# Four fused layers in one kernel: another port rule in its planner, shift by single elements, shared buffers, a maximum as Relu

## The chip, the core and the metric

The kernel runs on one core of a Trainium2 chip. A core has five engines that run their own instruction streams and wait for each other with semaphores: TensorE (PE, with weight loads shown apart as PEld), VectorE (DVE), ScalarE (ACT), GpSimd (POOL), and SyncE (SP), which here only issues transfers. The metric is the device time of one execution in microseconds; of several executions the median.

## What is computed

32 images `x` of 256 x 256 go through four layers, one after the other, each with its own weights. Cut to what matters:

```python
# layer 0: norm over the whole image, scale and shift by a condition, silu, two 256x256 products, residual
# layer 1: token norm with condition, attention of 16 heads with a bias per head, feed-forward of 1024
h = _ln(src) * (1.0 + scale) + shift
scores = einsum('bhqd,bhkd->bhqk', q / sqrt(16), k) + attention_bias      # fside, 32 x 16 x 256 x 256
scores = where(src_mask, -inf, scores); ctx = softmax(scores) @ v
x = x + (ctx @ Wo + bo)
return x + _gelu2(_ln(x) * g2 + beta2 @ W1 + b1) @ W2 + b2
# layer 2: a finite-difference step on the image as a grid
df = -gradv_Af + gradvv_Bf * 0.5
return maximum(f + df * dt, 0.0)
# layer 3: layer norm, causal attention of 16 heads, feed-forward with exact gelu, gated residual
x1 = x + attn(layernorm(x)); x2 = x1 + ff(layernorm(x1))
return x + gate_score * (x2 - x)
```

`_ln(x)` is `(x - mean) / sqrt(var + 1e-5)` along a row. All numbers are fp32.

## The kernel before

An image lies on chip as a tile of 128 partitions x 2 x 256. For each image three generators describe its work: `layer_0`, `layer_1`, and `layers_23` (the grid step and the last layer). They don't issue instructions. A recorder, class `Order`, notes each call with its engine, its operands and a due time (its rank); a step of a generator (`yield LAND` and the like) moves the due time on by so many microseconds times `PACE`, and `PERIOD`, `START`, `EDGE` and `SHIFT` place images, layers and steps against each other. When everything is noted, `arrange` plays the program through with a model of the engines: at each moment it gives each engine, among its units that are ready by the model, the one of the lowest rank. `emit` then issues all calls in the order of the planned starts. So the order on every engine is fixed in the program; the chip runs each engine's stream in that order. Work of two to three images is interleaved.

The model (lines 72 to 90 and `length`) has a duration for each form of instruction, the hop from one engine to another (`HOPS`, `OWNS`, and `SLACK`, a margin for TensorE), what a change of TensorE's shape costs (`TURN`, `FIRST`), how many PSUM banks scores, transposes and products may hold (`CAPS`), and the port: a unit marked `port` on VectorE can't run beside one on GpSimd. `record` sets the mark by the number of elements of the operands (16 and more).

The tiles that matter here:
- `sc`: scores of one head in PSUM. VectorE's fused operation adds the bias (`nb` in layer 1, prepared by GpSimd from the loaded `fside` and the mask; `causal` in layer 3), writes `pr` and the row's minimum `mn`. ScalarE turns `pr` into exponentials and sums them. TensorE transposes `pr` into `tr`, VectorE or ScalarE copies that to `pt`, and TensorE multiplies `pt` by the values. `pr` has six buffers for layer 1 (`pr1`) and six for layer 3 (`pr3`).
- `ctx_t`: the product with the values, copied by ScalarE, then multiplied by VectorE with the inverse sums, which GpSimd spreads (`wide`) and TensorE transposes. Then comes `L1wo` or `L3wo`.
- `token_norm` (used twice in each attention layer): VectorE takes mean and variance into `mv`, GpSimd computes `rstd` with a power, VectorE makes `shift` (-mean x rstd, two columns), ScalarE writes the normalised tile (`t` in the profile, as the tag `t2`), which TensorE transposes.
- `xm` (layer 1 after attention) and `d` (layer 3) have one buffer each; `d` is stored to memory at the end of an image.
- `x` at the end of layer 2 ("x3"): `dd * dt + f` on VectorE, then the maximum with zero, also on VectorE, then `token_norm`.

All transfers but a few at the start are issued by SyncE, in the planned order too.

Of the kernel before, what the change touches and what calls it, by code (L numbers as in the profile page):

```python
# [21 lines left out]
P = 128  # L22
# [19 lines left out]
PERIOD = 86.0  # L42
START = (-59.8, 0.0, 116.9)
PACE = (1.37, 1.22, 1.08)
EDGE = {(0, 0): -102.4, (0, 1): -3.5, (0, 2): 0.3, (1, 0): -29.2, (1, 1): -9.5, (1, 2): -3.3, (2, 0): -4.4, (2, 1): -1.3, (2, 2): 1.9, (3, 0): 7.5, (3, 2): 0.7, (4, 0): -2.3, (4, 1): 1.2, (4, 2): 0.6, (27, 0): 7.3, (27, 1): 1.5, (27, 2): 0.7, (28, 0): -2.3, (28, 1): 1.6, (28, 2): 4.6, (29, 0): 2.1, (29, 1): -0.7, (29, 2): -0.1, (30, 0): 0.1, (30, 1): 3.4, (30, 2): -0.3, (31, 0): 3.1, (31, 1): 3.6, (31, 2): -30.9}
SHIFT = (
    {0: -23.5, 1: -31.5, 2: -24.4, 3: -36.5, 4: -13.4, 5: -35.7, 6: -44.8, 7: -28.5, 8: 20.9},
    {0: -11.9, 1: -93.5, 2: -5.9, 3: 2.4, 4: 4.1, 5: 6.4, 7: -9.2, 8: 7.3, 9: -92.1, 11: 7.2, 12: 20.9,
     13: -0.6, 14: 4.6, 15: -3.0, 16: 12.9, 17: 7.8, 19: 5.4, 20: 7.9, 21: 35.0, 22: 16.8, 23: -7.6,
     24: -11.1, 25: -25.5, 26: -3.5, 27: -66.1, 28: -0.5, 29: -110.6, 30: -4.3, 31: -15.2, 32: -19.4,  # L50
     33: 1.6, 34: -0.4, 35: 12.9, 36: 0.6, 37: -15.0},
    {0: -3.0, 1: -43.2, 2: 3.0, 3: 26.5, 4: 23.8, 5: -31.8, 6: -42.4, 7: -14.5, 8: -8.2, 9: 6.5,
     11: 3.8, 12: 16.4, 13: -29.4, 15: -3.4, 16: 18.0, 17: -4.1, 18: 7.0, 19: 0.1, 20: 0.7, 21: -69.9,
     23: 8.3, 24: 7.8, 25: -0.5, 26: -13.8, 27: -43.4, 28: 14.4, 29: -5.3, 30: 25.3, 31: 1.7, 32: -8.7,
     33: -40.0, 34: 13.4, 35: -21.0, 36: -92.3, 37: -36.5, 38: -60.7, 39: 56.2, 40: -26.9, 41: 7.7},
    {0: -11.5, 1: 3.4, 2: -31.6, 3: -95.1, 4: 57.5},
)
# [7 lines left out]
class Order:  # L65
# [8 lines left out]
    SETUP = 15e3  # L74
    HOPS = {"act": 40.0, "dve": 40.0, "pool": 90.0, "pe": 60.0, "sync": 60.0}
    OWNS = {"act": 30.0, "dve": 30.0, "pool": 83.0, "sync": 30.0}
    TURN = 92.0
    FIRST = {(32, P): 107.0, (P, 32): 27.0}
    SLACK = 50.0
    SEEN = 165.0  # L80
    CAPS = {"sc": 6, "tr": 7, "mm": 6}
    EARLIER = {"sc": 28.7, "mm": -1.9, "tr": 6.1}
    STAY = 5.0
    PORT = 0.05
# [41 lines left out]
    def record(self, engine, call, method, args, kwargs):  # L126
# [11 lines left out]

        inner = [a for a in ins if math.prod(n for _, n in a.ap[1:]) >= 16]
        sources = sum(a.space != PSUM for a in inner)  # L140
        alone = method in ("tensor_scalar", "tensor_copy") and all(a.space != PSUM for a in outs)
        x["port"] = bool(inner) and (engine == "pool" or engine == "dve" and (sources > 1 or sources == 1 and alone))
        x["lead"] = 142.0 if engine == "pool" else x["length"][2] if engine == "dve" else 0.0
# [24 lines left out]
    def length(self, engine, method, outs, ins, args, kwargs):  # L168
# [5 lines left out]
        if engine == "pe":  # L174
            lhs = kwargs.get("lhsT")
            rows = 32 if lhs is not None and lhs.partition_size() <= 32 else P
            cols = 32 if outs[0].partition_size() <= 32 else P
            slot = (lhs.start_partition(), outs[0].start_partition()) if lhs is not None else (0, 0)
            passes = 1 if method == "transpose" or kwargs.get("is_transpose") else 2
            one = max(free(outs[0]) / 1.2 + 2.3, 109.0) if free(outs[0]) > 16 else 70.0  # L180
            return one * passes, (rows, cols), slot
        if method == "dma_start":
            return sum(math.prod(k for _, k in a.ap) for a in outs) * 4
        if engine == "dve":
            lead = 137.0
            if method == "reciprocal":
                return 120 + 8.3 * n, 40 + 8.3 * n, lead
            if method == "tensor_tensor_reduce":
                return 235 + 1.05 * n, 73 + 1.05 * n, lead
            if method == "tensor_scalar":  # L190
                a = (265 if columns else 150) + (1.06 if psum else 0.55) * n
                lead = 257.0 if columns else lead
            elif method == "scalar_tensor_tensor":
                a = 205 + 1.05 * n
                lead = 195.0
            else:
                a = 148 + 1.05 * n
            return a, a - 80, lead
        if engine == "act":
            if method == "copy":  # L200
                a = 157 + 0.84 * n
            else:
                a = (255 if columns else 200) + 0.84 * n + (93 if columns > 1 else 0)
                if "accum_out" in kwargs:
                    a += 115
            return a, a - 95, self.TABLES.get(args[2] if len(args) > 2 else None)
        if method == "tensor_tensor":
            a = 640 if n <= 4 else 185 + 2.13 * n
        else:
            a = 185 + 0.86 * n + (70 * columns if columns > 1 else 0)  # L210
        return a, a - 40 if n > 4 else a + 10

    def arrange(self):
# [47 lines left out]
        banks = defaultdict(lambda: (None, 0.0))  # L261
        table = None

        def may(u, at):
# [11 lines left out]
        while todo:  # L276
# [6 lines left out]
            for e in self.ENGINES:  # L283
# [6 lines left out]
                for k, heap in ready[e].items():  # L290
# [5 lines left out]
                    if e == "pe" and units[u][2][0]["length"][1] != shape:  # L296
                        rank += self.STAY
                    if k[1]:
                        rank += self.PORT * max((pool_end if e == "dve" else dve_end) - now, 0.0)
# [10 lines left out]
                for x in units[u][2]:  # L310
                    if e == "pe":
                        one, its_shape, slot = x["length"]
                        if its_shape != shape:
                            t = max(t, pe_end + self.TURN)
# [5 lines left out]
                        x["start"] = pe_last = t  # L320
                        done = t + one + (0.0 if slot in slots else self.FIRST.get(shape, 0.0))
                        slots[slot] = done
                        pe_end = max(pe_end, done)
                        t = done if shape == (P, P) else t + 6.6
                        done += self.SEEN
                    elif x["method"] == "dma_start":
# [3 lines left out]
                    else:  # L330
                        x["start"] = now
                        more = max((pool_end if e == "dve" else dve_end) - now - x["lead"], 0.0) if x["port"] else 0.0
                        more = max([more] + [t - now for f, t in map(banks.__getitem__, x["banks"]) if f != e])
                        if e == "act" and x["length"][2] not in (None, table):
                            table = x["length"][2]
                            more += self.TABLE
                        done, t = (now + a + more for a in x["length"][:2])
                        if x["port"] and e == "pool":
                            pool_end = done
# [74 lines left out]
def kernel(ctx: ExitStack, tc: tile.TileContext, io, out, n_batch=B):  # L414
# [23 lines left out]
    causal = ctile("causal", [P, S])  # L438
    edge = ctile("edge", [P, 3, 2, 4])

# [128 lines left out]

    small = sb.tile([P, 16, B], F32, tag="pr1", name="encodings", bufs=6)  # L570
    x0, r0, n0, a0, enc, x1f, r1, n1, a1, emb0, emb1 = (small[:, i] for i in range(11))
# [35 lines left out]

    small = sb.tile([P, 4, 4, B], F32, tag="pr1", name="hidden0", bufs=6)
    h1, zh, th, h1s = (small[:, i] for i in range(4))
    small = sb.tile([P, 4, 4, B], F32, tag="pr1", name="hidden1", bufs=6)  # L610
    h2, zh1, th1, embs = (small[:, i] for i in range(4))
# [70 lines left out]
    def loads():  # L682

        load_rest(l1, "L1", "g2", "beta2")
        yield LAND

        sync.dma_start(edge, io["c_edge"].rearrange("p (k e x) -> p k e x", k=3, e=2))
        a1 = sb.tile([P, C2, D], F32, tag="l2", name="a1", bufs=4)
# [37 lines left out]
    def token_norm(x, tag="t2", bufs=3):  # L726

        st = sb.tile([P, C2, 6], F32, tag="st", name="st", bufs=4)
        mv = sb.tile([P, C2, 2], F32, tag="mv", name="mv", bufs=4)
# [4 lines left out]
        shift = sb.tile([P, C2], F32, tag="shift", name="shift", bufs=4)  # L734
        dve.scalar_tensor_tensor(shift, mv[:, :, 0], -1.0, r, ALU.mult, ALU.mult)
        xn = sb.tile([P, C2, D], F32, tag=tag, name=tag, bufs=bufs)
# [46 lines left out]
    def attention(n, w, h_t, get_in1, causal_keys):  # L783
# [32 lines left out]
        def scores(u):  # L816
# [17 lines left out]
            for i in range(HQ):  # L834
                pr = sb.tile([P, sum(keys)], F32, tag=f"pr{n}", name="pr", bufs=6)
                prs[u].append(pr)
# [160 lines left out]
    def layer_1(b, res):  # L997
# [35 lines left out]
        for c in range(C2):  # L1033
            with order.together():
                for k in range(C2):
                    pe.matmul(pm[:, c, :], lhsT=ctx_t[:, k, c * P : (c + 1) * P], rhs=l1.wo[:, k, :], start=k == 0, stop=False)
                for k in range(C2):
# [3 lines left out]
                    )  # L1041
        xm = sb.tile([P, C2, D], F32, tag="xm", name="xm", bufs=1)
        dve.tensor_tensor(xm, pm, bcast(l1.bo, C2), ALU.add)
# [9 lines left out]
    def layers_23(b, res):  # L1053
# [55 lines left out]
        dve.scalar_tensor_tensor(x, dd, dt_b[:, b : b + 1], f, ALU.mult, ALU.add)  # L1109
        dve.tensor_scalar(x, x, 0.0, None, ALU.max)  # L1110
        xn = token_norm(x)
        yield NORM
        h_t = ff_input(xn, l3_g1, l3_beta1)
        d = sb.tile([P, C2, D], F32, tag="d3", name="d3", bufs=1)
        add_row(d, x, l3.bo)
# [71 lines left out]
```

## Time and profile before

| | |
|---|---|
| runs shown | 2708.65, 2708.8, 2711.2 us; median 2708.8 |
| the profiled execution | 2711.45 us, of it a span of 2709.7 us |
| mean granted TensorE clock | 0.988 |
| 0 to 67 us | PE busy 33.65, DVE 37.41, ACT 12.69, POOL 22.36; PE clock 0.80; DMA 227 GB/s |
| 1200 to 1500 us | PE busy 296.86, DVE 249.45, ACT 224.06, POOL 172.01; PE clock 1.00; DMA 60 GB/s |
| 2643 to 2710 us | PE busy 50.87, DVE 22.67, ACT 28.27, POOL 5.78; PE clock 0.85; DMA 8 GB/s |

A matmul of fp32 takes two passes (two records); a transpose takes one. Ends of matmuls in the profile are modelled: two that follow each other overlap. So a busy TensorE is not one at its peak, and a short wait between two matmuls can be hidden by the modelled end of the first. "Idle before" is the time in which an engine had nothing, and the arrow names what ended it. All instructions are recorded by one helper and have one line (L365), so they are told apart by their tiles. In the profile numbers are left out of names: `L3w,hid` is the second product of layer 3's feed-forward, `h_t,L3w` the first.

The program's order of instructions can be read engine by engine without a profile, of a changed kernel too; where the prediction speaks of the built order, that is meant.

### The profile page before, as it was taken

What the parts mean: (1) busy time and instruction counts of PE and PEld (TensorE: products, weight loads), DVE (VectorE), ACT (ScalarE), POOL (GpSimd) and SP (SyncE); (2) the same over time, 40 slices, a digit from 0 to 9 for tenths busy, and PEclk for the clock granted to TensorE, in tenths of its full rate; (3) what the DMA queues carried; (4) which work ended last, traced back from release to release, by engine and by line L of the source; (5) the groups of instructions that cost most, each with busy time, mean ns of one, the idle gap of its engine ahead of it and who ended that gap; (6) DMA issues with size and microseconds to landing.
All of it is one profiled execution on the core that took longest, in us unless ns stands there. A gap on an engine that the chain in (4) does not pass through costs nothing.

```text
span 2709.7 us, 60241 instructions
## 1 busy us (share of the span) xinstructions
PE 2616.1 (97%) x20462; PEld 2121.2 (78%) x20462; DVE 2166.8 (80%) x7499; ACT 1929.2 (71%) x6120; POOL 1570.6 (58%) x1960
## 2 busy tenths in 40 slices
PE   5999999999999999999999999999999999999987
PEld 3778788888788878788878788878787878888775
DVE  5887878888888888888888888888887887888753
ACT  1767777877767877767877767877777877777854
POOL 3855666555666555666555666555666555666420
PEclk7999999999999999999999999999999999999998
DMA  6411122211122211122211122211122211122100
GB/s 225 122 54 54 59 64 68 69 56 49 49 72 68 68 55 46 53 72 68 69 54 46 53 72 68 68 54 46 55 70 68 68 56 42 56 68 64 44 5 8
DMA packets 177062, 169.67 MB, mean 63 GB/s; under 512 B 19514, under 2 KB 175220, under 8 KB 176756
## 3 DMA queue, kind: packets, MB, share of 16 engines
q1 hardware_dynamic: 176720, 165.82, 19.9%
q8 instruction: 163, 2.67, 0.4%
q14 instruction: 143, 1.17, 0.1%
q10 hardware_dynamic: 36, 0.01, 0.0%
HBM read 157.40 MB, written 8.39 MB: 61 GB/s over the span
## 4 chain that ended last, share of the span: by engine, by line
PE 61%; POOL 25%; DVE 6%; issue 4%; ACT 2%; DMA 1%; SPq 0%; ACTq 0%; POOLq 0%; DVEq 0%
PE mm L365 45%; POOL nb L365 10%; PE tr L365 9%; PE sc L365 7%; POOL rstd L365 4%; POOL d L365 2%; POOL offset L365 2%; POOL mask_f L365 2%; DVE pr L365 1%; POOL cmf L365 1%; POOL b0f L365 1%; DVE st L365 1%; POOL a0f L365 1%; POOL cpf L365 1%; POOL small L365 1%
## 5 line engine op out<-in xcount | busy, mean ns | idle before, releaser
L365 ACT ACTIVATE pr<-pr,mn 128x256 f32<-128x256 f32 (+1 forms) x2048 | 967.9, 479 | 153.3 <-DVE mn L365 142.0
L365 POOL TENSOR_TENSOR nb<-mask_f,nb 128x512 f32<-128x512 f32 x512 | 683.9, 1355 | 60.7 <-DMA nb<-in_fside_Bx16xSxS_dram 46.6
L365 PE MATMUL tr<-ident,pr 128*128 128x128 f32 x3584 | 491.5, 275 | 8.1 <-ACT pr L365 2.5
L365 PEld LDWEIGHTS tr<-ident,pr 128*128 128x128 f32 x3584 | 416.4, 142 | 77.2 <-ACT pr L365 23.5
L365 DVE CUSTOM_DVE_ANT_0 pr<-sc,nb 128x256 f32<-128x256 f32 x1024 | 387.7, 417 | 90.0 <-PE sc L365 87.0
L365 ACT ACTIVATION_READ_ACCUMULATOR pr<-pr,mn 128x1 f32 x2048 | 397.1, 194 | 0.0
L365 DVE CUSTOM_DVE_ANT_0 pr<-sc,causal 128x128 f32<-128x128 f32 (+1 forms) x1024 | 309.5, 350 | 57.9 <-PE sc L365 40.7
L365 DVE COPY pt<-tr 128x512 f32<-128x512 f32 (+1 forms) x512 | 311.4, 615 | 45.8 <-PE tr L365 43.7
L365 POOL TENSOR_SCALAR hid<-hid 128x256 f32<-128x256 f32 x256 | 99.8, 405 | 373.1 <-ACT hid L365 372.9
L365 ACT COPY pt<-tr 128x512 f32<-128x512 f32 (+1 forms) x512 | 261.9, 528 | 56.6 <-PE tr L365 51.8
L365 POOL COPY wide<-rs 128x256 f32<-128x256 f32 x128 | 53.5, 418 | 414.5 <-DVE rs L365 384.4
L365 PE MATMUL sc<-k_t,nq 32*128 32x256 f32 (+1 forms) x4096 | 268.3, 374 | 0.0
L365 PE MATMUL mm<-h_t,L1w 128*128 128x256 f32 x1024 | 252.2, 386 | 0.7 <-DVE mn L365 0.4
L365 PE MATMUL mm<-h_t,L3w 128*128 128x256 f32 x1024 | 249.5, 388 | 1.8 <-DVE h_t L365 1.3
L365 PE MATMUL mm<-L3w,hid 128*128 128x256 f32 x1024 | 239.2, 387 | 10.2 <-ACT hid L365 10.2
L365 PE MATMUL mm<-L1w,hid 128*128 128x256 f32 x1024 | 243.4, 381 | 0.0
L365 PEld LDWEIGHTS mm<-L3w,hid 128*128 128x128 f32 x1024 | 193.2, 194 | 36.2 <-ACT hid L365 11.5
L365 PEld LDWEIGHTS sc<-k_t,nq 32*128 32x128 f32 x4096 | 162.5, 184 | 69.6 <-issue 27.8
L365 PEld LDWEIGHTS mm<-h_t,L3w 128*128 128x128 f32 x1024 | 188.7, 194 | 32.0 <-issue 6.1
L365 PEld LDWEIGHTS mm<-h_t,L1w 128*128 128x128 f32 x1024 | 182.7, 190 | 38.6 <-DVE pt L365 6.0
L365 PEld LDWEIGHTS mm<-L1w,hid 128*128 128x128 f32 x1024 | 184.9, 190 | 21.8 <-issue 1.6
L365 ACT ACTIVATE t<-x,shift,rstd 128x256 f32<-128x256 f32 x128 | 70.0, 593 | 160.6 <-DVE shift L365 160.2
(173 smaller groups left out, 5060.4 us busy)
## 6 DMA issues: line engine op xcount, KB each, us to landing
nb<-in_fside_Bx16xSxS_dram SPq DMA_DIRECT2D x512, 256.0 KB
x<-in_x_dram SPq DMA_DIRECT2D x32, 256.0 KB
out_dram<-d SPq DMA_DIRECT2D x32, 256.0 KB
mask<-in_mask_Bx1xSxS_bk_dram SPq DMA_DIRECT2D x32, 64.0 KB
L1w<-in_L_cond_W_dram SPq DMA_DIRECT2D x2, 1024.0 KB
L3w<-in_L_cond_W_dram SPq DMA_DIRECT2D x2, 1024.0 KB
l0w<-in_L_cond_W_dram SPq DMA_DIRECT2D x1, 1024.0 KB
g_b<-in_L_cond_B_grid_dram SPq DMA_DIRECT2D x3, 256.0 KB
```

The source lines that it names most:

```text
L365: call(*args, **kwargs)
```

## The change

In the kernel's own work:

```diff
@@ token_norm
-        st = sb.tile([P, C2, 6], F32, tag="st", name="st", bufs=4)
+        st = sb.tile([P, C2, 6], F32, tag="st", name="st", bufs=2)
...
-        dve.scalar_tensor_tensor(shift, mv[:, :, 0], -1.0, r, ALU.mult, ALU.mult)
+        for c in range(C2):
+            dve.tensor_scalar(shift[:, c : c + 1], mv[:, c, 0:1], r[:, c : c + 1], -1.0, ALU.mult, ALU.mult)
@@ attention
-                pr = sb.tile([P, sum(keys)], F32, tag=f"pr{n}", name="pr", bufs=6)
+                pr = sb.tile([P, sum(keys)], F32, tag="pr", name="pr", bufs=10)
@@ layer_1
-        xm = sb.tile([P, C2, D], F32, tag="xm", name="xm", bufs=1)
+        xm = sb.tile([P, C2, D], F32, tag="xm", name="xm", bufs=3)
@@ layers_23
-        dve.tensor_scalar(x, x, 0.0, None, ALU.max)
+        act.activation(x, x, AF.Relu)
...
-        d = sb.tile([P, C2, D], F32, tag="d3", name="d3", bufs=1)
+        d = sb.tile([P, C2, D], F32, tag="xm", name="d3", bufs=3)
```

The small tiles of the start (`encodings`, `hidden0`, `hidden1`) and `edge`, which had a place of its own, move to the common tag `pr`. In the planner:

```diff
-        inner = [a for a in ins if math.prod(n for _, n in a.ap[1:]) >= 16]
-        sources = sum(a.space != PSUM for a in inner)
-        alone = method in ("tensor_scalar", "tensor_copy") and all(a.space != PSUM for a in outs)
-        x["port"] = bool(inner) and (engine == "pool" or engine == "dve" and (sources > 1 or sources == 1 and alone))
+        inner = [n for n in (math.prod(n for _, n in a.ap[1:]) for a in ins if a.space != PSUM) if n > 1]
+        alone = method in ("tensor_scalar", "tensor_copy") and all(a.space != PSUM for a in outs) and max(inner, default=0) > 4
+        x["port"] = bool(ins) and (engine == "pool" or engine == "dve" and (len(inner) > 1 or len(inner) == 1 and alone))
...
-    HOPS = {"act": 40.0, "dve": 40.0, "pool": 90.0, "pe": 60.0, "sync": 60.0}
-    OWNS = {"act": 30.0, "dve": 30.0, "pool": 83.0, "sync": 30.0}
+    HOPS = {"act": 36.0, "dve": 36.0, "pool": 90.0, "pe": 54.0, "sync": 60.0}
+    OWNS = {"act": 34.0, "dve": 34.0, "pool": 83.0, "sync": 30.0}
...
-    FIRST = {(32, P): 107.0, (P, 32): 27.0}
-    SLACK = 50.0
-    SEEN = 165.0
-    CAPS = {"sc": 6, "tr": 7, "mm": 6}
-    EARLIER = {"sc": 28.7, "mm": -1.9, "tr": 6.1}
-    STAY = 5.0
+    FIRST = {(32, P): 107.0, (P, 32): 27.0, (P, P): 107.0}
+    APART = 120.0
+    SLACK = 0.0
+    SEEN = {(32, P): 165.0, (P, 32): -16.0, (P, P): 165.0}
+    CAPS = {"sc": 4, "tr": 6, "mm": 8}
+    EARLIER = {"sc": 34.4, "mm": -2.7, "tr": 5.5}
+    STAY = 0.0
+    FRESH = 1.0
+    PAIR = 0.0
```

So a small operation now counts as a user of the port when it streams two operands of more than one element, and one with a single element does not. `APART` is a gap between certain GpSimd operations, `FRESH` a rank penalty for beginning whole-array two-pass matmuls behind a turn, and the durations of a few small operations in `length` are changed. The tables `START`, `PACE`, `EDGE` and `SHIFT` get other numbers throughout. As every order in the program comes from this plan, the order on all engines changes, the transfers' too. There are 128 more instructions: 96 on VectorE (128 second shifts less 32 maxima) and 32 on ScalarE.

## The prediction, made before the changed kernel ran

> **What bounds the kernel now.** I read the page first, then the engines' busy time by stretch, then who waited for whom on TensorE, and last the timeline around its longest repeated wait. The first lines below are the page's busy times and its chain of waits by engine.
>
> ```profile
> PE 2616.1 (97%) x20462; PEld 2121.2 (78%) x20462; DVE 2166.8 (80%) x7499; ACT 1929.2 (71%) x6120; POOL 1570.6 (58%) x1960
> ...
> PE 61%; POOL 25%; DVE 6%; issue 4%; ACT 2%; DMA 1%; SPq 0%; ACTq 0%; POOLq 0%; DVEq 0%
> ```
>
> TensorE is the bound. The chain gives POOL a quarter, but the list of TensorE's own waits hardly names POOL: only 0.4 us, for `wide`. POOL work lies beside TensorE's. What is left to win is TensorE's waits (us, times, longest):
>
> ```profile
> PE mm L365 <- DVE ctx_t L365: 19.6, 19, 1.7
> PE mm L365 <- ACT t L365: 12.2, 8, 3.7
> PE mm L365 <- ACT hid L365: 10.6, 4, 4.2
> PE mm L365 <- DMA x<-in_x_dram: 10.3, 3, 6.4
> ```
>
> The last three lie mostly in the first 70 and the last 110 us, where few images overlap. The first one repeats in the middle, once in most images, which follow each other at 81.3 us (the first `L1wo` matmuls start at 1278.74 and 1360.08). Three engines around one such wait, TensorE, VectorE, GpSimd in turn (start, us, engine, operation, idle before):
>
> ```profile
> 1278.74 0.68 PE L365 MATMUL mm<-L1wo,ctx_t 128*128 128x256 f32 x2
> 1280.46 0.70 PE L365 MATMUL mm<-L1wo,ctx_t 128*128 128x256 f32 x2 [1.03 <-DVE ctx_t L365]
> ```
> ```profile
> 1278.86 1.21 DVE L365 SCALAR_TENSOR_TENSOR shift<-mv,rstd 128x2 f32<-128x2 f32 x1 [0.41 <-POOL rstd L365]
> 1279.99 0.41 DVE L365 TENSOR_TENSOR ctx_t<-ctx_t,mm 128x256 f32<-128x256 f32 x1
> 1280.32 1.25 DVE L365 TENSOR_SCALAR x<-x 128x512 f32<-128x512 f32 x1
> ```
> ```profile
> 1278.80 2.49 POOL L365 TENSOR_TENSOR nb<-mask_f,nb 128x512 f32<-128x512 f32 x2
> ```
>
> A `shift` of two numbers per partition took 1.21 us, because it began 0.06 us after the first of two GpSimd `nb` and ended when that did, 1.25 us on. Behind it stood the `ctx_t` product, and behind that TensorE. The next lines price such operations (min/median/max ns; in the ScalarE row: busy us, mean ns, then idle time before).
>
> ```profile
> L365 DVE SCALAR_TENSOR_TENSOR shift<-mv,rstd x128: 141/160/1219, 52.1 to 2678.4; 128x2 f32<-128x2 f32 x128
> ```
> ```profile
> L365 DVE TENSOR_SCALAR dev<-mv,mean x64: 174/197/215, 20.8 to 2468.1; 128x1 f32<-128x1 f32 x64
> ```
> ```profile
> L365 DVE TENSOR_SCALAR x<-x x32: 426/1240/1396, 146.2 to 2636.7; 128x512 f32<-128x512 f32 x32
> ```
> ```profile
> L365 ACT ACTIVATE th<-y 128x512 f32<-128x512 f32 x32 | 20.2, 630 | 62.6 <-DVE y L365 57.9 <-PE mm L365 4.7
> ```
>
> **The change, part by part.** All sums start from the profiled execution: span 2709.7, its run 2711.45, the median of the runs 2708.8. So I add the parts to the span and take off 0.9 at the end.
>
> *The shift.* The form of the new operations is that of `dev`: one element, one pointer. None of 64 took over 215 ns, though GpSimd was busy 58% of the time. Two cost 2 x 0.197 = 0.39 us against a mean of 0.429 now (54.9 us over 128), and they don't wait for `nb`. The built order of the changed kernel also puts no shift ahead of this `ctx_t` product: it follows the update of `x`, and TensorE does `l_wout` (8 passes of 0.216 = 1.7 us) more between `wide` and `L1wo`: 5.2 us of cover where there were 3.5. I count the wait as gone: 19.6 us, and 19 x 0.16 that the modelled end of the matmul ahead hides (a pass of 256 columns is shown 0.38 long, though the next can start 0.22 later): −22.7. Bounds: 0 if something else holds the product; −26 with the smaller waits of the same place.
>
> Here a page speaks against the form. The Trainium skill, "SBUF — State Buffer", section "Who interferes with whom", says that `tensor_scalar` can enter a two-port mode and then contends with GpSimd, while a second SBUF input contends with GpSimd's reads. The old `shift` with its two inputs is what it describes; by it the new one might still wait, up to 1.2 us each. The `dev` row says no. By the page alone the gain from the form would be 0, and only the changed place in the order would be left.
>
> *The maximum as Relu.* VectorE loses 32 x 0.98 = 31.5 us (mean of `x<-x`), ScalarE gets 32 x 0.63 = 20.2. Its order puts the Relu, in 25 images, right behind the copy of `ctx_t`, where the profile shows ScalarE idle for 4.85 us before the normalisation. On the way from `x` to its normalisation it is 0.35 us shorter, and TensorE rarely waits there, so I take 0. Bounds: −0.35 x 32 = −11 if all of it were on the path, and against a free port (0.426) 0.2 x 32 = +6.5. If the idle time were gone, the Relu would stand behind the 1.9 us Gelu and delay `t`, `L3wq` and the next scores.
>
> The Trainium skill, "ScalarE: Activation LUTs", section "Rules for kernel authors", says to use VectorE and not ScalarE for relu and max. The trace's 426 ns minimum agrees, its median of 1240 beside GpSimd does not. By the page this part would be the +6.5.
>
> *Common buffers.* `xm` and `d` share three buffers instead of one each: GpSimd waited 41.5 us, 30 times, for the output transfer of `d`; none of it reached TensorE, so 0. The probability tiles are 10 in all instead of 6 and 6. VectorE waited 9.9 us for transposes to free the causal ones; a common pool may cut that or spread it. Taken: 0; bounds −4 (those of its waits that TensorE could feel) and +38 (rival two).
>
> *TensorE's own order.* Scores and values use a quarter of the array; each turn between these and whole-array work costs 0.093 us, the first two-pass matmul after it 0.104 and the first transpose 0.056 (spacings of starts in this trace). Turns go from 694 to 717 (+2.1), two-pass matmuls behind a turn from 156 to 63 (−9.7), transposes from 157 to 274 (+6.6): −1.0.
>
> *Head.* TensorE and VectorE:
>
> ```profile
> 30.17 1.12 PE L365 MATMUL mm<-ident,x 128*128 128x128 f32 x4 [6.41 <-DMA x<-in_x_dram]
> 31.08 3.53 PE L365 MATMUL mm<-th,l_win 128*128 128x256 f32 x8
> ```
> ```profile
> 27.68 0.69 DVE L365 SCALAR_TENSOR_TENSOR th<-th,y 128x512 f32<-128x512 f32 x1 [0.69 <-ACT th L365]
> ```
>
> The first image's `l_win` could start at 28.4 us but stands behind the second image's transposes, whose `x` is the 37th issue on SP. In the changed order `x` is the 16th; behind it come `L3wq`, `L3wk`, `L3wv`, `causal` and then the fourteen small `as_rows` loads, which all move five issues later. TensorE now meets the `as_rows` transpose just ahead of `l_win`. It had its data at 22.2; five issues of 0.51 us each are 2.6 us, or 1.125 MB at about 350 GB/s (the rate around there) 3.3 us: 25.5, still before 28.4. `L1wq`, moved too, is used at 56.9 only. So −2.7; bounds −5 (the next images' steps move up too) and 0.
>
> *Tail.* TensorE once the last image is alone with the one before it:
>
> ```profile
> 2621.27 1.18 PE L365 MATMUL mm<-ident,t 128*128 128x128 f32 x4 [3.00 <-ACT t L365]
> 2623.09 6.39 PE L365 MATMUL mm<-h_t,L3w 128*128 128x256 f32 x16 [0.64 <-DVE h_t L365]
> ...
> 2639.31 3.39 PE L365 MATMUL mm<-L3w,hid 128*128 128x256 f32 x8 [4.15 <-ACT hid L365]
> ```
>
> In the changed order the stencil matmuls stand ahead of `L3wo` and that `ident,t`, and `L3wq`, `L3wk`, `L3wv` and three score groups ahead of that `L3w,hid`: work of the last image fills these 7.8 us. Priced with the spacings above, 60 us of matmuls follow the last image's `L1w,hid` instead of 52, so its chain starts 8 us of TensorE work earlier. The chain itself, 92 us to the end, gets more work between its links. I take −5; bounds −8 and +3.
>
> *Covers that shrink.* TensorE's work between a producer and its user in a middle image, before and after: `L3w,hid` 5.8 to 4.5 (the tail row needs 4.15 + 0.16 = 4.3 behind an idle ScalarE); `L3wo` 1.8 to 0.9 (behind the last `wide` the trace needs 0.38 to the product, 0.41 for it, 0.06 to TensorE: 0.85); `rows_t` 3.0 to 1.7; `L1w,hid` 6.9 to 4.9. All just suffice where the engine between is free, and the planner gives up 50 ns of margin per hop to TensorE. I take 0.2 us per image, 32 x 0.2 = +6.4, nearer to "they suffice"; bounds 0 and one late `nb`, 1.2 x 32 = +38. `L3wq` keeps its 1.7 us cover and its wait. Against that, the `t` waits in the middle (12.2 less 3.0 and 3.75 in the tail and 1.91 in the head: 3.5) follow a shift; I take −2.
>
> Sum: 2709.7 − 22.7 − 1.0 − 2.7 − 5 + 6.4 − 2 = 2682.7; less 0.9 gives **2682**.
>
> **The rivals.**
>
> *One: the wait moves.* The covers cost not 0.2 but 0.9 us per image: 2682 + 0.7 x 32 = 2704, about no change. For it: four covers have under 0.2 us to spare or lost 1.3 to 2 us. Against: the steady images of the trace show hardly another wait than the `ctx_t` one, with the same kind of tight order. That the new shift still waits for `nb` ends here too.
>
> *Two, slower: the common probability buffers.* A unit of attention takes four tiles and holds them until TensorE has transposed them. Two units of layer 1 and one of layer 3 ask for 12; with 10, two score tiles per overlap wait until the other layer's transposes are through, and each delays its `pr` product (0.42), its exponential (0.50) and the sum's read (0.19): 1.1 us. If two such delays per image reach TensorE, it is 2 x 1.1 x 32 = +70: 2752; with one, 2717. It decides from 0.85 us per image on (27 us gained, over 32). For it: VectorE's 9.9 us of waiting for transposes already. Against: transposes run all the time, and the cover of most of them is over 3 us.
>
> *Three: more than the sum.* Summed over all matmuls between 135 and 2575 us, starts come 57 us later than the spacings above would have them; 23 of that are counted above and 6 belong to `L3wq`. If half of the other 28 (waits behind `mn`, `hid`, `dev`) goes too, and the covers cost nothing: 2682 − 6 − 14 (half of the 28) = 2662.
>
> **How the numbers follow.** The forecast (2668 to 2696) has 0.55, three (to 2650) 0.24, one 0.11, two 0.10. The range is 2652 to 2704: it leaves out rival two and the ends of the others. A measurement of this kernel tells 0.2%, 5.4 us, from no change. Faster, below 2703.4: forecast, three and half of one, 0.84. Same: 0.06. Slower: rival two, 0.10.
>
> **What would show it.** Right: the `ctx_t` wait on TensorE falls from 19.6 to under 3 us, `shift` shows no duration over 0.3 us, the middle images follow each other at 80.0 to 80.5 us instead of 81.3, `l_win` starts before 29.5, and no wait of 3 us stands between the last two images' feed-forwards. Wrong: shifts of over 1 us (the port), TensorE waiting for `hid`, `rows_t` or `L3wo`'s `ctx_t` once per image (one), or VectorE's `pr` waiting for transposes by more than 30 us (two).

## The result, and the profile after

| | before | after |
|---|---|---|
| median of the runs compared | 2709.39 us (2708.65 to 2711.2, 4 runs) | 2693.98 us (2690.93 to 2695.3, 4 runs) |
| ratio after / before | | 0.9941, interval 0.9923 to 0.9958 |
| profiled execution, its span | 2711.45, 2709.7 us | 2690.93, 2689.1 us |
| mean granted TensorE clock | 0.988 | 0.988 |

The change gained 15.4 us where 27 were forecast. The page of the kernel after, busy times and the chain of waits by engine:

```profile
PE 2611.3 (97%) x20462; PEld 2121.4 (79%) x20462; DVE 2123.5 (79%) x7595; ACT 1951.9 (73%) x6152; POOL 1559.1 (58%) x1960
...
PE 87%; ACT 5%; DVE 4%; DMA 1%; POOL 1%; issue 1%; SPq 0%; ACTq 0%; POOLq 0%; DVEq 0%
```

POOL has left the chain (25% to 1%). TensorE's own waits in the kernel after (us, times, longest):

```profile
PE tr L382 <- ACT pr L382: 14.5, 35, 1.7
PE mm L382 <- ACT t L382: 10.4, 3, 5.1
PE mm L382 <- DVE th L382: 9.5, 3, 5.2
PE mm L382 <- ACT hid L382: 7.3, 5, 4.2
...
PE mm L382 <- DVE ctx_t L382: 0.3, 1, 0.3
```

The wait for `ctx_t` is down from 19.6 us to 0.3, as the forecast had it. In its place stands a wait that the prediction didn't name: TensorE's transposes of probabilities (`tr`) wait for ScalarE's exponentials (`pr`). The two groups of instructions that the change gives another form (min/median/max ns, first the shift, then the Relu):

```profile
L382 DVE TENSOR_SCALAR shift<-mv,rstd x256: 121/205/218, 48.1 to 2657.9; 128x1 f32<-128x1 f32 x128
L382 ACT ACTIVATE x<-x x32: 612/631/632, 138.3 to 2611.6; 128x512 f32<-128x512 f32 x32
```

No shift is long any more: the longest takes 218 ns, where before one took 1219.

Where the new wait sits shows in one image of the middle, kernel after, timelines of TensorE and ScalarE (start, us, engine, operation, idle before):

```profile
1287.55 0.33 PE L382 MATMUL tr<-ident,pr 128*128 128x128 f32 x1
1288.31 0.44 PE L382 MATMUL tr<-ident,pr 128*128 128x128 f32 x2 [0.43 <-ACT pr L382]
```
```profile
1283.52 0.63 ACT L382 ACTIVATE th<-y 128x512 f32<-128x512 f32 x1 [0.16 <-DVE y L382]
1285.32 0.37 ACT L382 COPY L3v<-mm 128x256 f32<-128x256 f32 x1 [1.17 <-PE mm L382]
1285.71 1.28 ACT L382 ACT_TABLE_LOAD   x1
1287.00 0.40 ACT L382 ACTIVATE pr<-pr,mn 128x128 f32<-128x128 f32 x1
```

An `ACT_TABLE_LOAD` of 1.28 us, which makes ScalarE ready for the exponential after other functions, stands once per image directly ahead of an exponential, here the first of layer 3's attention. In the kernel after, a copy of values (`L3v`) stands ahead of that load, and the copy waits 1.17 us for TensorE. So ScalarE idles, then copies, then loads, and only then makes the first exponential. The same place before:

```profile
1292.32 0.84 ACT L365 ACTIVATE k_t<-mm,cols 128x256 f32<-128x256 f32 x2 [2.13 <-PE mm L365]
1293.17 1.28 ACT L365 ACT_TABLE_LOAD   x1
1294.54 0.40 ACT L365 ACTIVATE pr<-pr,mn 128x128 f32<-128x128 f32 x1
```

Here the load follows `k_t` at once and runs while TensorE is still at the values, whose first copy comes behind the first exponential. Nothing in the diff speaks of tables: the planner's model, before and after, puts tanh (`th`) into the exponential's set alone and so has the load paid at `th`; in the trace `th` ran without a load and the exponential behind it needed one. A model that doesn't see the load can put it anywhere; before's plan has it ahead of the values in all 31 images without knowing of it.

To sum TensorE's waits, I took the median spacing between starts for each pair of neighbouring matmul forms, the same for all kernels, and added up what exceeds it by 0.06 us or more: the *late starts*. Over the whole run they are 136.7 us before and 114.7 after; the difference, 22.0, is that of the spans, 20.6, within 1.4. So, within what this way of summing can tell (a few us), TensorE's own work is unchanged and what was won are waits. A wait that comes in most images of one kernel goes in part into the medians and is then missing from the sum; e7 below is such a case.

By stretches, from the first `L1wo` matmul of one image to that of another: it comes at 90.91 us instead of 95.74 for the first image, but at 385.01 instead of 385.14 for the fifth; from the fifth to the 29th image 1938.03 instead of 1951.63 us, on to the last 241.26 instead of 241.53, and from there to the end 124.8 instead of 131.4. The gain is 13.6 in the middle and 6.6 at the end.

### The profile page after: what moved, and what is told of

It is laid out like the page before. It is cut to its first block, busy times and chain, and to the rows that moved or that the text cites. A ratio compares the mean times of both kernels' runs of the same rounds, so it can differ in the third digit from the quotient of the medians.

```text
span 2689.1 us, 60107 instructions
## 1 busy us (share of the span) xinstructions
PE 2611.3 (97%) x20462; PEld 2121.4 (79%) x20462; DVE 2123.5 (79%) x7595; ACT 1951.9 (73%) x6152; POOL 1559.1 (58%) x1960
## 3 DMA queue, kind: packets, MB, share of 16 engines
q1 hardware_dynamic: 176720, 165.82, 20.1%
## 4 chain that ended last, share of the span: by engine, by line
PE 87%; ACT 5%; DVE 4%; DMA 1%; POOL 1%; issue 1%; SPq 0%; ACTq 0%; POOLq 0%; DVEq 0%
PE mm L382 65%; PE tr L382 14%; PE sc L382 9%; ACT pr L382 2%; ACT L382 1%; DVE pr L382 1%; DMA nb<-in_fside_Bx16xSxS_dram 1%; ACT L3v L382 1%; DVE pt L382 1%; POOL nb L382 0%; DVE gd L382 0%; ACT hid L382 0%; DVE st L382 0%; ACT t L382 0%; DMA l_win<-in_L_cond_W_in_dram 0%
## 5 line engine op out<-in xcount | busy, mean ns | idle before, releaser
L382 PE MATMUL tr<-ident,pr 128*128 128x128 f32 x3584 | 499.5, 278 | 17.5 <-ACT pr L382 14.5
L382 PEld LDWEIGHTS tr<-ident,pr 128*128 128x128 f32 x3584 | 402.8, 141 | 122.8 <-ACT pr L382 57.4
L382 DVE CUSTOM_DVE_ANT_0 pr<-sc,causal 128x128 f32<-128x128 f32 (+1 forms) x1024 | 302.6, 352 | 75.5 <-PE sc L382 73.3
L382 PE MATMUL mm<-h_t,L1w 128*128 128x256 f32 x1024 | 243.6, 380 | 0.0
L382 PE MATMUL mm<-h_t,L3w 128*128 128x256 f32 x1024 | 240.6, 385 | 1.3 <-DVE h_t L382 1.3
L382 POOL COPY wide<-rs 128x256 f32<-128x256 f32 x128 | 64.6, 505 | 283.2 <-DVE rs L382 220.2
L382 PEld LDWEIGHTS mm<-h_t,L1w 128*128 128x128 f32 x1024 | 185.3, 190 | 22.5 <-issue 1.3
```

The source lines that it names most:

```text
L382: call(*args, **kwargs)
```

## The experiments

All were compared with the kernel before on the same chip: 2707.83 us (2706.41 to 2712.46) for the first four, 2708.81 for the next three, 2707.9 for the three after, 2710.07 for the last. "Table behind values" counts the images, of 31 with a load there, in which the exponential's table load stands behind the first copy of values; "late transposes" are the late starts of TensorE's transposes that wait for `pr`, from 135 to 2575 us.

| kernel | median us | ratio to before (interval) | table behind values | late transposes us | all late starts us |
|---|---|---|---|---|---|
| before | 2708 to 2710 | 1 | 0 | 0.4 | 136.7 |
| after | 2693.98 | 0.9941 (0.9923 to 0.9958) | 21 | 21.7 | 114.7 |
| e1 | 2680.2 | 0.9897 (0.9884 to 0.9911) | 0 | 0.4 | 106.0 |
| e2 | 2701.27 | 0.9974 (0.9964 to 0.9984) | 21 | 21.5 | 122.4 |
| e3 | 2694.48 | 0.995 (0.9937 to 0.9962) | 21 | 21.7 | 117.4 |
| e4 | 2671.95 | 0.9869 (0.9855 to 0.9882) | 0 | 3.6 | 94.6 |
| e5 | 2694.12 | 0.995 (0.9937 to 0.9962) | 21 | 23.3 | 115.4 |
| e6 | 2707.52 | 0.9996 (0.9987 to 1.0005) | 14 | 12.2 | 130.9 |
| e7 | 2747.6 | 1.0144 (1.013 to 1.0158) | 21 | 20.0 | 146.3 |
| e8 | 2707.76 | 1.0002 (0.9993 to 1.001) | 0 | 0.4 | 135.0 |
| e9 | 2656.39 | 0.9812 (0.9799 to 0.9825) | 1 | 0.2 | 84.9 |
| e10 | 2659.33 | 0.9819 (0.9806 to 0.9833) | 1 | 0.9 | 87.4 |
| e11 | 2691.92 | 0.9936 (0.9923 to 0.995) | 23 | 20.1 | 115.2 |

**e1: the shift's form alone.** The kernel before with its order; only the shift becomes two operations.

```diff
-        dve.scalar_tensor_tensor(shift, mv[:, :, 0], -1.0, r, ALU.mult, ALU.mult)
+        def single(out, mean, scalar, rstd, op0, op1):
+            for c in range(C2):
+                nc.vector.tensor_scalar(out[:, c : c + 1], mean[:, c : c + 1], rstd[:, c : c + 1], scalar, op0, op1)
+        order.record("dve", single, "scalar_tensor_tensor", (shift, mv[:, :, 0], -1.0, r, ALU.mult, ALU.mult), {})
```

> The kernel before, every engine's order as before, but each shift is written as two operations of one element. Theory (the two-element shift waits for GpSimd's port and holds up the ctx_t product behind it): the shift takes 2 x 0.2 us instead of 1.21 beside an nb, the product ends 0.8 us earlier, TensorE's wait at the second L1wo falls from 1.03 to about 0.25 us, middle images follow each other at 80.5 us instead of 81.3, and the run takes about 2689 us (0.8 x 25 = 20 less). Rival (the gain of the whole change is the new order's, and the shift's form does nothing by itself): still 81.3 us per image, 2709 us.

It gains 27.6 us (2707.83 to 2680.2), more than the whole change. The shifts of e1 and TensorE's wait for `ctx_t`:

```profile
L738 DVE TENSOR_SCALAR shift<-mv,rstd x256: 195/205/216, 51.6 to 2648.0; 128x1 f32<-128x1 f32 x128
```
```profile
PE mm L365 <- DVE ctx_t L365: 3.3, 10, 1.7
```

Everything else in the change together, with this form already there, costs 13.8 us (2680.2 to 2693.98). Kernel after and e1 were timed in different sessions, in which before took 2709.39 and 2707.83 us; counted from these, it costs 12.2. Differences between after and a variant carry this uncertainty of 1 to 2 us throughout.

**e2: the new order with the old shift.** The kernel after; the first record of the pair issues the old operation on two numbers, the second issues nothing.

```diff
-            dve.tensor_scalar(shift[:, c : c + 1], mv[:, c, 0:1], r[:, c : c + 1], -1.0, ALU.mult, ALU.mult)
+            def both(*args, c=c, shift=shift, mv=mv, r=r):
+                if c == 0:
+                    nc.vector.scalar_tensor_tensor(shift, mv[:, :, 0], -1.0, r, ALU.mult, ALU.mult)
+            order.record("dve", both, "tensor_scalar", args, {})
```

> The changed kernel, every engine's order as there, but the shift is again one operation of two elements. Theory (in the new order no ctx_t product stands behind a shift): some shifts take up to 1.2 us again, the ctx_t wait on TensorE stays under 3 us, and the run takes 0 to 8 us more than the changed kernel, 2694 to 2702. Rival (the form alone carries the gain): the 0.8 us per image come back somewhere, 2714.

It is 7.3 us slower than after. The long shifts are back, 51 of 128 over 0.3 us:

```profile
L756 DVE SCALAR_TENSOR_TENSOR shift<-mv,rstd x128: 97/161/1251, 49.0 to 2669.2; 128x2 f32<-128x2 f32 x128
```

Yet TensorE's wait for `ctx_t` stays at 0.3 us; what grew is its wait for `t`, 10.4 to 14.0. So the new order and the new form each cure the same `ctx_t` wait: the form is worth 27.6 us in the old order and 7.3 in the new.

**e3: the maximum back on VectorE**, in the new order, at the Relu's place (the operation `tensor_scalar` with max, recorded for ScalarE and issued on VectorE).

```diff
-        act.activation(x, x, AF.Relu)
+        on_dve = lambda out, x, relu: nc.vector.tensor_scalar(out, x, 0.0, None, ALU.max)
+        order.record("act", on_dve, "activation", (x, x, AF.Relu), {})
```

> The changed kernel, but the maximum with zero is VectorE's again, at the place where the plan has the Relu. Theory (the Relu's place is off TensorE's path, as the prediction had it at 0): 0 to 5 us more than the changed kernel, though VectorE is busy 30 us longer; the maximum takes 0.43 to 1.4 us again. Rival (the Relu saves 0.35 us or more of a chain that ends at TensorE): 11 us more or over, 2705.

2694.48 against 2693.98 us: within the spread of the runs the Relu neither costs nor gains.

**e4: the table load early.** The kernel after, with one exponential of a single column ahead of the first copy of values in each image, so that the load falls there.

```diff
+            def copy(dst, src, par=par):
+                if n == 3 and par == 0:
+                    nc.scalar.activation(warm[:, 1:2], warm[:, 0:1], AF.Exp)
+                nc.scalar.copy(dst, src)
-            act.copy(dst, src)
+            order.record("act", copy, "copy", (dst, src), {})
```

> The changed kernel, and ScalarE does one exponential of a single column, used by nobody, ahead of layer 3's first copy of the values, so that the table for exponentials is loaded while ScalarE waits for that product. Theory (the new wait of 0.92 us per image at the first causal transposes is the table load of 1.28 us, which stands behind that copy): the wait goes, middle images follow each other at 79.7 to 79.9 us instead of 80.65, and the run takes about 2672 us (0.85 x 26 = 22 less than 2694). Rival (the transposes wait for the exponentials themselves, which only queue up): no change, 2694; or another wait comes in its place, 2685 to 2694.

It gains 22.0 us on the kernel after (22.5 on e3, which was timed beside it and takes as long as after). ScalarE in a middle image of e4, then TensorE's wait for the exponentials:

```profile
1272.00 0.84 ACT L382 ACTIVATE k_t<-mm,cols 128x256 f32<-128x256 f32 x2 [2.94 <-PE mm L382]
1273.00 0.63 ACT L382 ACTIVATE th<-y 128x512 f32<-128x512 f32 x1 [0.16 <-DVE y L382]
1273.65 1.28 ACT L831 ACT_TABLE_LOAD   x1
1274.94 0.20 ACT L831 ACTIVATE warm<-warm 128x1 f32<-128x1 f32 x1
```
```profile
PE tr L382 <- ACT pr L382: 4.6, 17, 0.8
```

The load now overlaps the 1.2 us in which ScalarE would wait for the values. Of the 65 loads of the program 21 moved to the new instruction, just the 21 that stood behind the values: 22.0 / 21 = 1.05 us for each.

**e5: the same additional instruction, but late.** The two lines of e4 change places: copy first, then the exponential.

> The kernel after with the same orders, and the same single-column exponential per image on ScalarE as in e4, now right behind layer 3's first copy of values instead of ahead of it. Nothing is left out. Theory (what e4 gained came from the table load standing ahead of the copy): the load is behind the copy again, the causal transposes wait for pr as in after (about 22 us in some 35 waits or more), and the dummy adds some 0.2 us per image to the same chain: 2690 to 2702, ratio to before 0.993 to 0.997. Rival (the additional instruction or the shifted timing of ScalarE did it, wherever it stands): as e4, 2665 to 2680.

2694.12 us, as after, and TensorE's wait is there again:

```profile
PE tr L382 <- ACT pr L382: 17.1, 56, 1.0
```

It is the load's place that gained in e4, not the additional instruction.

**e6: before's port rule**, everything else as after, planned again.

```diff
-        inner = [n for n in (math.prod(n for _, n in a.ap[1:]) for a in ins if a.space != PSUM) if n > 1]
+        inner = [a for a in ins if math.prod(n for _, n in a.ap[1:]) >= 16]
...
```

> The kernel after, planned again with before's port rule (a small operation is never a user of the port); tables, buffers, shift form and Relu are after's. Nothing is left out. In its built order the table load and the first two causal exponentials stand ahead of layer 3's first copy of values. Theory (the load's place is what the new plan loses, the rule by itself is worth little once the shift is single): the causal transposes' wait for pr is under 8 us, shift stays under 0.3 us, and the time is near e4's, 2660 to 2690, with an unknown of 10 us either way from the other changes of order. Rival (the rule keeps small operations clear of GpSimd and is worth its place): small two-operand operations of over 1 us come back ahead of TensorE's inputs, and it is slower than after, 2700 to 2725.

A miss: 2707.52 us. The sentence on the built order was true of 17 images only; in 14 the load still stands behind the values, and the late transposes are 12.2 us. The time lies in the rival's range, but its reason isn't there: no group of small operations that every image has is longer than in after (the 256 shifts have a mean of 207 ns in both). Late starts are 16.2 us more than in after though the late transposes are 9.5 less, so some 26 us of other waits came in, spread over many places (behind `h_t`, `t`, `pt`, `gd` and others). What the rule is worth can't be told from this: another rule gives another plan, under tables of numbers that were chosen for the first.

**e7: before's buffers**, everything else as after, planned again (`pr1` and `pr3` of six, `xm` and `d3` of one, `st` of four).

```diff
-                pr = sb.tile([P, sum(keys)], F32, tag="pr", name="pr", bufs=10)
+                pr = sb.tile([P, sum(keys)], F32, tag=f"pr{n}", name="pr", bufs=6)
...
```

> The kernel after, planned again with before's buffers (six and six probability tiles, one each of xm and d, edge with a place of its own); tables, port rule, shift form and Relu are after's. Nothing is left out. In its built order the table load stands behind layer 3's first copy of values, as in after. Theory (the common buffers neither cost nor save much; the load's place decides): the causal transposes wait for pr by 14 us or more, GpSimd waits for d's output transfer again without TensorE feeling it, 2685 to 2715. Rival (the common pool of probabilities costs turns): faster than after by over 10 us, under 2680. Rival (the common pool saves what the plan needs): VectorE's or GpSimd's waits for buffers reach TensorE, over 2720.

2747.6 us, the third reading. It has new TensorE waits, in some 20 images each, ahead of the stencil (14.4 us in 18 waits) and in layer 3's feed-forward (`hid`, 11.8 us in 23); GpSimd waits again for the output transfer of `d`, 20.6 us, and VectorE's `pr` for transposes, 19.4, where neither is among the kernel after's waits. Its span is 51.6 us longer than after's and its late starts only 31.6 more: waits that come as often as those ahead of the stencil are in the medians. That the common buffers cost turns finds no support: VectorE's `pr` waits for no transposes in after, and e7 isn't faster. How much they save is as confounded with the new plan as in e6.

**e8: which property of the new shift avoids the wait?** As e1, but with the old operation on single elements.

```diff
-                nc.vector.tensor_scalar(out[:, c : c + 1], mean[:, c : c + 1], rstd[:, c : c + 1], scalar, op0, op1)
+                nc.vector.scalar_tensor_tensor(out[:, c : c + 1], mean[:, c : c + 1], scalar, rstd[:, c : c + 1], op0, op1)
```

> The kernel before with all orders as before, the shift as two single-element operations as in e1, but of the old operation (scalar_tensor_tensor, both inputs single elements) instead of tensor_scalar with a pointer. Nothing is left out. Theory (the number of elements decides whether a small operation waits beside GpSimd): no shift over 0.3 us, TensorE's wait for ctx_t under 4 us, 2677 to 2685 as e1. Rival (the operation with two inputs from SBUF decides): shifts of over 1 us come back beside nb, each of the pair may wait, TensorE waits for ctx_t by 15 us or more, 2700 to 2720.

The theory fell: 2707.76 us, no gain at all. The shifts of e8, then VectorE and GpSimd at the known place, then TensorE's wait:

```profile
L738 DVE SCALAR_TENSOR_TENSOR shift<-mv,rstd x256: 142/154/1253, 51.6 to 2677.0; 128x1 f32<-128x1 f32 x128
```
```profile
1279.65 1.28 DVE L738 SCALAR_TENSOR_TENSOR shift<-mv,rstd 128x1 f32<-128x1 f32 x2 [0.41 <-POOL rstd L365]
1280.85 0.41 DVE L365 TENSOR_TENSOR ctx_t<-ctx_t,mm 128x256 f32<-128x256 f32 x1
```
```profile
1279.58 2.49 POOL L365 TENSOR_TENSOR nb<-mask_f,nb 128x512 f32<-128x512 f32 x2
```
```profile
PE mm L365 <- DVE ctx_t L365: 20.8, 19, 1.7
```

A pair of single-element operations with two inputs from SBUF waits for `nb` just as one of two elements did. The name of the operation is not the reason: the kernel before has the same operation with one streamed input in PSUM (`mm`) and one in SBUF, on 512 elements. 27 of the 32 begin while an `nb` runs, and none is prolonged.

```profile
L365 DVE SCALAR_TENSOR_TENSOR y<-mm,mean,gamma_t x32: 708/711/752, 19.8 to 2416.0; 128x512 f32<-128x512 f32 x32
```

What counts is the second streamed input from SBUF: as the pointer of a `tensor_scalar` it isn't waited for, as a second operand it is. After's port rule goes by the number of elements and would call e8's pair free; it serves this kernel because its shift has the other form as well.

**e9 to e11: plans that know the tables.** The planner of after is told that tanh runs with the exponential's table and with gelu's; its numbers `START`, `PACE`, `EDGE`, `SHIFT`, `CAPS`, `EARLIER` and margins are then searched anew (e9 and e10: two starts of the search). e11 is the same search, for as long, without being told.

```diff
-    TABLES = {AF.Sin: 0, AF.Tanh: 1, AF.Exp: 1, AF.Gelu: 2}
+    TABLES = {AF.Sin: (0,), AF.Tanh: (1, 2), AF.Exp: (1,), AF.Gelu: (2,)}
...
-                        if e == "act" and x["length"][2] not in (None, table):
-                            table = x["length"][2]
+                        if e == "act" and x["length"][2] is not None and table not in x["length"][2]:
+                            table = x["length"][2][0]
```

> The kernel after, planned again by a planner that is told which activation functions share a table on this chip (tanh runs with the table of exp and with that of gelu, so the load falls on the first exponential), and with START, EDGE, SHIFT and the other planner settings searched anew under that model. No additional instruction, buffers, port rule, shift and Relu as in after. Nothing is left out. In its built order the exponential's table load stands ahead of layer 3's first copy of values in all images but the last. Theory: the causal transposes' wait for pr falls from 14.5 to under 6 us and the time is 2655 to 2685. Rival (what a new plan wins at one place it loses at others, as in e6): pr waits fall, but other waits on TensorE take their place, 2685 to 2710.

> As e9, from another start of the search (with another number of PSUM banks for transposes and products and other margins). Nothing is left out. In its built order too the table load stands ahead of layer 3's first copy of values in all images but the last. Theory: pr waits under 6 us, 2655 to 2685, within 12 us of e9. Rival: the spread between two plans of the same kind is larger than what the load's place is worth, over 2690 or more than 20 us from e9.

> Control for e9 and e10: the kernel after, its START, EDGE, SHIFT and the other planner settings searched anew for as long and in the same way, but with after's own account of the tables. The plan it found ends as early by its model as e9's by its own. Nothing is left out. In its built order the table load stands behind layer 3's first copy of values in 23 of 31 images. Theory (knowing the tables is what e9 and e10 gained by): the causal transposes wait for pr as in after, about 1.0 us per such image, and the time is 2672 to 2692. Rival (the new search alone did it): 2650 to 2665, without such waits.

e9 takes 2656.39 us and e10 2659.33, the best of all: 51.5 us under before, 37.6 under after (e9). e11 takes 2691.92, no better than after beyond the spread of the runs. So this search by itself found next to nothing on the chip; with the corrected table model it found 35.5 us more. Of that the late transposes are 19.9 (20.1 to 0.2). The spans of e11 and e9 differ by 25.0 us between the fifth and the 29th image and by 12.1 ahead of these and behind; why the part beyond the late transposes was won isn't shown, and with one search as control some of it may be the search's luck. ScalarE in a middle image of e9, then TensorE's wait for the exponentials in e9 and in e11:

```profile
1270.84 0.63 ACT L376 ACTIVATE th<-y 128x512 f32<-128x512 f32 x1 [0.16 <-DVE y L376]
1271.49 1.28 ACT L376 ACT_TABLE_LOAD   x1
1272.79 0.40 ACT L376 ACTIVATE pr<-pr,mn 128x128 f32<-128x128 f32 x1
```
```profile
PE tr L376 <- ACT pr L376: 4.7, 7, 1.2
```
```profile
PE tr L376 <- ACT pr L376: 13.3, 29, 1.9
```

e9 has as many loads as after, 65, none removed; the exponential's have only moved ahead of the copies of values.

## Why the prediction was right, and where it was off

The direction and the range were right, the gain was 12 us too large (2682 against 2693.98). Some of that was luck: a loss of about 22 us that the prediction didn't see was partly made good by 5 us more from the shift's form and by what the rest of the plan brought. By its steps:

- *The shift*: right, in mechanism and in both its reasons. The form alone takes the wait away (e1), and so does the changed place (e2). Its worth, 22.7, is the low side of e1's 27.6: behind the long shifts waited not only `ctx_t` but smaller things too. From 390 to 2575 us the late starts behind `ctx_t` fell in e1 by 15 us, those behind `t` by 3, all of them by 26. The reading of the row `dev` held where a page seemed to speak against it. That page, the Trainium skill's "SBUF — State Buffer", section "Who interferes with whom", says two things that the runs now tell apart. A second input from SBUF contends with GpSimd's reads: e8 shows it at one element, 1253 ns at most. For `tensor_scalar` it refers to the conditions of the two-port mode, which the prediction passed over, so that the page did not speak against the form after all. "VectorE: DVE Perf Modes", section "Mode 2×_2P — use both read ports for one tensor", has the outermost dimension of more than one element split between the two ports; a single element per partition has none. The 256 shifts of e1 agree: 66 of them begin while an `nb` runs, and none takes over 216 ns.
- *The maximum as Relu*: 0 forecast, 0 found (e3).
- *Common buffers*: 0 forecast. Rival two (turns for ten probability tiles) didn't come: VectorE's `pr` waited for transposes by 10.5 us before and doesn't in after, nor does GpSimd for the output of `d` (41.5 before), and e7 with the old buffers isn't faster. What the buffers are worth by themselves isn't settled.
- *TensorE's own order*: −1.0 forecast; spans and late starts differ by 1.4 in the other direction. Nothing, within what this way of summing can tell.
- *Head*: the step itself came as described (`l_win` at 27.44 instead of 31.08), but it is worth 0.1 us, not 2.7, by the fifth image. At the first `L1wo` the gain was still 4.8; one wait then took most of it back: `l_wout` at 143.94 us stands 5.19 us for `th` of the next image. The forecast followed the chain to its first link and counted what was won there as won for good.
- *Tail*: −5 forecast, −6.6 found; but e1, with the old order, has 4.2 of it as well (127.1 us from the last `L1wo`), so the new order, the reason that was given, is needed for the rest only. The wait for `hid` between the last two images fell from 4.15 to 0.49 as described, but that for `t` rose from 3.00 to 5.13, so "no wait of 3 us" was wrong.
- *Covers that shrink*: the step that failed. It priced 0.2 us per image, 6.4 in all, at four named places. There the loss was about half of that: between 390 and 2575 us `L3w,hid` has 6.5 us of late starts instead of 3.1, and `rows_t`, `L3wo` and `L1w,hid` have next to none. But the cover that broke was a fifth one, ahead of the causal transposes, by 21.7 us, or 1.0 in each of 21 images. The prediction looked at TensorE's cover in instructions and at the engine between as "free"; it didn't follow ScalarE's own order at that place, where the built order of the changed kernel shows the load behind the copy.

Counted from e1, then: −27.6 for the form, some +22 for the late loads, and −8.3 for the rest of the new plan (e4 against e1): 13.9 us, what after is under the before of those runs. The forecast was closest to the kernel without the late loads, e4, 2671.95. Rival one ("the wait moves", 0.9 us per image) had the right kind and price of loss; it had it at other places and without a gain beside it, and the time came between the two. The middle images follow each other at 80.65 us, a little above the 80.0 to 80.5 that was said.

## What to carry to other kernels

A table load belongs to the order of its engine like any other instruction of 1.28 us: when an order changes, look where each load lands and whether the engine is idle there; a copy that waits, placed ahead of it, turns it from hidden to paid for. Where GpSimd works beside it, a small per-partition operation on VectorE that stands ahead of TensorE's input is best written with its second input as a pointer scalar. And a planner is only as good as its account of the machine: one wrong entry left open where the loads land, and in after that cost about 22 us (e4), more than the 8 that the new rule, the new buffers and the new numbers together brought on top of the shift (e4 against e1).

## What was not expected of the hardware

- Tanh ran without a table load right after gelu, and the exponential behind it had the load ahead of it, 28 times before and 27 after, of 31 such loads (at the others no `th` stands between the gelu and the load). "ScalarE: Activation LUTs", section "Table sets: the hidden batching unit", lists tanh with exp and doesn't name it beside gelu; by that listing alone the load would be at `th`, as the planner had it. All 65 loads are of 1.28 us, the first exponential starting 0.01 us behind the load in after; the 2.7 us which that page gives for a switch, a drain included, isn't seen here.
- The wait beside GpSimd doesn't go away with size: a shift of one element with two inputs from SBUF takes up to 1253 ns, of two elements up to 1219.
- The same sort of price in every plan: about 1 us of late transposes per load behind the values (21.7 for 21, 20.0 for 21, 12.2 for 14, 20.1 for 23, 0.2 and 0.9 for 1, in after, e7, e6, e11, e9 and e10).
